# A selective scan in pairs of tiles: where a Mamba layer keeps its states, and in how many instructions it makes them

## The chip, the cores and the metric

The kernel runs on one core of a Trainium2 chip. The core has five engines that work side by side, each from its own queue in order: TensorE (PE, matrix products into PSUM), VectorE (DVE), ScalarE (ACT, functions such as Exp), GpSimd (POOL) and SyncE (SP, which here issues DMAs). PSUM has eight banks; one bank holds 512 f32 numbers for each of 128 partitions. The metric is the device time of one execution in microseconds (us). Times below are the median of several executions; a profile is of one execution.

## What is computed

The program is a stack of eight residual blocks over 32 sequences of 256 tokens with 128 features. The change touches the first block alone, a Mamba layer that runs in two directions (forward f, backward b). Cut to what matters here:

```python
xc = silu(causal_conv(in_proj(layernorm(x))));  z = ...
dt, Bm, Cm = split(xc @ xp_w.T)              # 16 states
delta = softplus(dt @ dtp_w.T + dtp_b);  A = -exp(A_log)
def step(h, inp):                            # h: 256 channels x 16 states
    dA = exp(d_t[..., None] * A)
    h = dA * h + (d_t * u_t)[..., None] * B_t[:, None, :]
    y = sum(h * C_t[:, None, :], axis=-1)
    return h, y
y = (y + xc * Dskip) * silu(z);  return y @ out_w.T
```

The backward direction does the same over the reversed sequence. All arithmetic is f32. The seven blocks behind it (two feed-forward blocks with experts, attention, and so on) are the same in both kernels.

## The kernel before

Tokens lie along the free axis, features along partitions. A chunk is 512 tokens (two sequences of 256), there are 16 chunks, and a chunk in one direction is a unit, so there are 32 units. The generator `unit` holds the whole work of one unit and gives up control at each `yield`; `pipeline` starts a new unit every 16 steps and moves all active units on by one step in turn, oldest first. A unit spends its first 24 steps on preparation (normalisation, convolution on PE, Silu, the projections, softplus by way of Abs, Exp and Ln, the gate) and then 16 steps on the recurrence, with three more to finish. So in any stretch of 16 steps one unit is in its recurrence while the next is being prepared.

256 channels times 16 states are 4096 rows, that is, 32 tiles of 128 partitions by 512 tokens. Two loops run over them: `h` (2 halves of the channels) and `g` (4 groups), and in a group `k` counts 4 tiles. For one tile:

- ACT makes the exponentials `dA` (L608), 510 of 512 elements. The first element of each of the two sequences stays zero, which resets the running state there. `dA` is one of three PSUM banks in turn (`dAs`, zeroed once at those places).
- POOL makes `dBu`, the product of delta times u (`widedu`) and B (L612), into one of four SBUF buffers.
- DVE runs the recurrence as one scan instruction (L621): state = dA * state + dBu along the 512 tokens.
- The states are multiplied by C. The states of tiles 0 and 1 lie side by side in a two-bank PSUM tile `h2`, and one DVE instruction multiplies both (L623, 1024 elements). Tile 2 uses `h2` again and is multiplied by DVE alone (L631). Tile 3 has its states in SBUF (`hs`), and POOL multiplies it (L569); all of the operands of POOL in this kernel lie in SBUF.
- PE sums four states to a channel with a 128x32 matrix (L574), one quarter of the output partitions for each `k`, into the one bank `yps`, after a first product with `skip` (L572). When a half is complete, `gated` multiplies `yps` by the gate on DVE (L590).

The PSUM banks of this stage are: 3 for `dAs`, 2 for `h2`, 2 for the preparation (`m`), 1 for `yps`.

What sets the order: the program is written as a sequence, and a planner (the tile framework) turns it into one queue for each engine. It keeps the data dependences and the reuse of buffers, sets the semaphores, and where an instruction is not ready by its own estimate it issues a later one of the same engine that is. `behind_scans` (through `issue_after`) keeps a few DVE instructions of the preparation and `gated` behind the last scan written. `summed` for group g is written after the second tile of group g+1, so the product of POOL stands in the text behind two further `dBu`. In step terms, one step holds two tiles.

SP issues the loads of the recurrence: `bc` (B and C, spread over partitions), and `wide` (delta and delta times u) in two halves, the first six steps ahead and the second at the second group of the first half.

## Time and profile before

| | us |
|---|---|
| median of 3 executions | 6238.78 (6236.38 to 6243.42) |
| the profiled execution | 6234.39 |
| its span, first to last instruction | 6232.7 |
| first scan starts / last scan starts (from the span's start) | 77.7 / 2052.8 |
| scans in that stretch | 1024, in 32 units |
| from one unit's first scan to the next one's, mean of units 2 to 31 | 62.06 |

How to read the profile's lines: a page has the busy time of each engine, then the span in 40 equal slices with the busy share in tenths. In a table of groups a row has the source line, the engine, the operation, what it writes and reads with shapes, the count, the total busy time and the mean duration in ns of one instruction, and then the idle time of its engine just ahead of it with what ended that idle time. A row of waits says which engine and tile waited for which, the total in us, how many times, and the longest. A row of the timeline has a start in us, a duration in us, and "x2" where two alike are merged. Durations on DVE and ACT overlap by a little where an instruction starts before the one ahead of it has quite ended.

### The profile page before, as it was taken

How to read it: one execution, taken by the hardware profiler on the slowest of the kernel's cores; microseconds unless marked ns; L12 is line 12 of the kernel's file. 1: busy time of each engine (PE TensorE's matmuls, PEld its weight loads, DVE VectorE, ACT ScalarE, POOL GpSimd, SP SyncE). 2: the span in 40 equal slices, each digit the busy share in tenths (PEclk: the TensorE clock that was granted, in tenths of full speed). 3: DMA queues.
4: the chain of work that ended last, by engine and by line, in shares of the span. 5: the costliest groups of instructions: out<-in, count | busy, mean ns of one | idle time of the engine just before them, and what ended most of it. 6: DMA issues, size and time to landing. Idle time of an engine off the chain costs nothing. (4 is left out here: it accounts for less than half of the span.)

```text
span 6232.7 us, 73938 instructions
## 1 busy us (share of the span) xinstructions
PE 5356.8 (86%) x25850; PEld 2792.6 (45%) x25922; DVE 4117.2 (66%) x7006; ACT 2710.2 (43%) x4424; POOL 3289.4 (53%) x3074
## 2 busy tenths in 40 slices
PE   6777777777777799999998888897998999997997
PEld 2222222222221466965544444445884444443886
DVE  5998999989989554044555555655665666665565
ACT  4665666666655354344434444342221333333221
POOL 5888888888888564044634444443332333333332
PEclk9888988888988899598989999998998999998998
DMA  3333333333332740000000000004550000000555
GB/s 148 123 123 116 123 116 123 116 123 116 126 112 109 304 185 1 1 1 1 1 1 10 9 8 8 11 8 129 186 172 19 20 16 18 18 11 12 188 188 189
DMA packets 190421, 512.13 MB, mean 82 GB/s; under 512 B 22177, under 2 KB 75169, under 8 KB 164961
## 3 DMA queue, kind: packets, MB, share of 16 engines
q1 hardware_dynamic: 172192, 468.00, 21.1%
q0 software_dynamic: 17280, 35.69, 1.7%
q8 instruction: 205, 3.36, 0.2%
q10 hardware_dynamic: 576, 3.71, 0.2%
q14 instruction: 168, 1.37, 0.1%
HBM read 359.93 MB, written 147.38 MB: 81 GB/s over the span
## 5 line engine op out<-in xcount | busy, mean ns | idle before, releaser
L612 POOL TENSOR_TENSOR dBu<-widedu,bcB 128x512 f32<-128x512 f32 x1024 | 1294.8, 1284 | 249.9 <-DVE h L621 162.0
L621 DVE TENSOR_TENSOR_SCAN h<-dA,dBu 128x512 f32<-128x512 f32 x768 | 942.5, 1227 | 119.8 <-ACT dA L608 30.4
L574 PE MATMUL yps<-pr,cst_t 128*32 128x512 f32 x2048 | 579.9, 645 | 244.8 <-POOL pr L569 102.7
L936 POOL TENSOR_SCALAR_AFFINE_SELECT e<-e 128x2048 f32<-128x2048 f32 (+1 forms) x256 | 343.3, 1353 | 597.2 <-ACT e L1047 386.1
L1412 POOL DMA_INDIRECT rows_out<-y,goes x284 | 271.8, 957 | 559.9 <-DVE y L1410 464.2
L1000 DVE TENSOR_REDUCE nm<-st 128x2 f32<-128x512 f32 x512 | 324.3, 684 | 268.5 <-PE st L996 267.4
L608 ACT ACTIVATE dA<-widedelta,Af 128x510 f32<-128x510 f32 x512 | 348.5, 688 | 300.9 <-DVE h L621 222.0
L608 ACT ACTIVATE dA<-widedelta,Ab 128x510 f32<-128x510 f32 x512 | 345.0, 686 | 272.7 <-DVE h L621 209.5
L1187 ACT ACTIVATE s<-s 128x512 f32<-128x512 f32 x284 | 179.0, 630 | 578.3 <-DVE s L1186 309.2
L574 PEld LDWEIGHTS yps<-pr,cst_t 128*32 128x32 f32 x2048 | 86.8, 112 | 704.8 <-POOL pr L569 228.0
L315 POOL TENSOR_TENSOR rstd<-var,cst_t 128x4 f32<-128x4 f32 x128 | 130.0, 1016 | 516.2 <-DVE var L313 514.4
L781 POOL TENSOR_TENSOR comb<-comb,ye 128x512 f32<-128x512 f32 x224 | 284.8, 1275 | 182.0 <-DVE ye L780 75.2
L1060 ACT ACTIVATE e<-st 128x512 f32<-128x512 f32 x512 | 272.0, 598 | 184.5 <-PE st L1056 154.8
L569 POOL TENSOR_TENSOR pr<-hs,bcC 128x512 f32<-128x512 f32 x256 | 334.4, 1306 | 13.7 <-DVE hs L621 13.7
L621 DVE TENSOR_TENSOR_SCAN hs<-dA,dBu 128x512 f32<-128x512 f32 x256 | 308.3, 1204 | 48.8 <-ACT dA L608 47.3
L1301 POOL DMA_INDIRECT rows_in<-xt,slot x256 | 253.6, 991 | 119.0 <-issue 98.7
L623 DVE TENSOR_TENSOR pr<-h,bcC 128x1024 f32<-128x1024 f32 x256 | 309.8, 1210 | 8.5 <-PE yps L574 0.5
L1188 DVE TENSOR_TENSOR hh<-s,u_ps 128x512 f32<-128x512 f32 x284 | 195.4, 688 | 172.0 <-ACT s L1187 168.0
L1393 PE MATMUL g_ps<-xb,gu 128*128 128x256 f32 x1136 | 302.6, 389 | 3.6 <-ACT xb L1376 2.3
L1402 PE MATMUL yps<-dn,hh 128*128 128x128 f32 x2272 | 291.5, 276 | 5.9 <-DVE hh L1188 5.8
L1393 PE MATMUL u_ps<-xb,gu 128*128 128x256 f32 x1136 | 293.3, 381 | 0.0
L1402 PEld LDWEIGHTS yps<-dn,hh 128*128 128x128 f32 x2272 | 282.8, 192 | 15.3 <-DVE hh L1188 7.8
(353 smaller groups left out, 11248.5 us busy)
## 6 DMA issues: line engine op xcount, KB each, us to landing
gu<-in_gu SPq DMA_DIRECT2D x142, 512.0 KB, 3.7
rows_in<-zero SPq DMA_DIRECT2D x60, 1170.0 KB, 18.7
widedelta<-delta_d SPq DMA_DIRECT2D x64, 1024.0 KB, 5.5
widedu<-du_d SPq DMA_DIRECT2D x64, 1024.0 KB, 5.1
dn<-in_dn SPq DMA_DIRECT2D x142, 256.0 KB, 3.9
bcB<-xdbl_d SPq DMA_DIRECT2D x32, 1024.0 KB, 5.0
bcC<-xdbl_d SPq DMA_DIRECT2D x32, 1024.0 KB, 6.9
xr<-rows_in SPq DMA_DIRECT2D x142, 130.0 KB, 3.8
```

Source lines behind the costliest of these rows:

```text
L569: nc.gpsimd.tensor_mul(pr, hs, bc["C"][:, g, :])
L574: nc.tensor.matmul(yps[32 * k : 32 * k + 32, :], K("states"), pr, start=False, stop=(g == 3), skip_group_check=True, tile_position=(0, 32 ...
L608: nc.scalar.activation(two(dA)[:, :, 1:L], two(steps)[:, :, 1:L], AF.Exp, scale=A[s][:, at : at + 1])
L612: nc.gpsimd.tensor_mul(dBu, duw[:, k, :], bc["B"][:, g, :])
L621: scan[0] = nc.vector.tensor_tensor_scan(*views, 0.0, ALU.mult, ALU.add)
L623: nc.vector.tensor_mul(pr2, h2, bc["C"][:, g, :].unsqueeze(1).to_broadcast([P, 2, CH]))
L781: nc.gpsimd.tensor_add(comb, comb, ye)
L936: nc.gpsimd.affine_select(e, e, [[0, n], [sign, P]], ALU.is_gt, 0.0, base=base, channel_multiplier=-sign)
L1000: nc.vector.tensor_reduce(n1[:, x, 2 * r : 2 * r + 2], o.rearrange("p (j k) -> p j k", j=2), AX.X, ALU.max, negate=True,)
L1060: nc.scalar.activation(e0[:, r], o.rearrange("p (j k) -> p j k", j=2), AF.Exp)
L1393: nc.tensor.matmul(o[:, j, :], gu[:, at : at + P], xb, start=True, stop=True)
L1402: nc.tensor.matmul(yps[:, t, :], hh[:, k, t * P : (t + 1) * P], dn[:, k, :], start=(k == 0), stop=(k == FF // P - 1),)
```

## The change

The recurrence goes over 16 pairs of tiles in a unit, one pair a step, instead of 32 tiles, two a step.

- `dAs` is two tiles of two banks each (4 banks), where it was three of one bank. ACT still makes the exponentials of each tile with an instruction of its own.
- One scan runs over both tiles of a pair, 1024 elements. For three pairs of four it writes the states over the exponentials in PSUM. The zeros at the four sequence starts are overwritten by that, so ACT writes them anew with a small copy (`firsts(dA)`, 128x4) ahead of the exponentials of each pair whose buffer was overwritten: 12 times in a unit.
- For the fourth pair (`i % 4 == 3`) the scan writes the states over `dBu` in SBUF, and POOL multiplies them by C in place, one instruction of 1024 elements, written one step later, behind the next pair's `dBu`.
- DVE multiplies the other three pairs of four, 1024 elements each, out of PSUM into one of three `prod` buffers. `h2`, `hs` and the single products are gone. So of a unit's tiles, DVE multiplies 24 and POOL 8, as before.
- `dBu` is made by one POOL instruction for a pair, into one of four buffers of 1024 elements.
- PE's sums of a pair are written two steps after it; `gated` three steps after the last pair of a half. `yps` has two banks, one for each half.
- In the backward direction the pair lies in reverse order in `dA`, the scan reads `dBu` backward, and the multiplication reads the states backward.
- The second half of `wide` is loaded at pair 2, the same step as before. The banks are now 4, 2 and 2.

```diff
--- before.py
+++ after.py
@@ -403,9 +403,14 @@
 
 
 
-        dAs = [ps.tile([P, CH], F32, name=f"dA{k}", bufs=1) for k in range(3)]
-        for t in dAs:
-            nc.vector.memset(two(t)[:, :, 0:1], 0.0)
+        dAs = [ps.tile([P, 2, CH], F32, name=f"dA{k}", bufs=1) for k in range(2)]
+        nought = wp.tile([P, 4, 1], F32, name="nought")
+        nc.gpsimd.memset(nought, 0.0)
+
+        def firsts(dA):
+            return dA.rearrange("p k (b t) -> p (k b) t", b=2)[:, :, 0:1]
+
+        nc.vector.memset(firsts(dAs[1]), 0.0)
 
         def rows_of(ap, at, dims, n_rows):
 
@@ -559,84 +564,81 @@
                 yield
 
 
-
-            sums, ended = None, None
-            yps = None
-
-            def summed(h, g, prods, hs):
-                nonlocal yps, ended
-                pr = p2.tile([P, CH], F32, tag="prod", name="pr", bufs=4)
-                nc.gpsimd.tensor_mul(pr, hs, bc["C"][:, g, :])
-                if g == 0:
-                    yps = ps.tile([P, CH], F32, tag="y", name="yps", bufs=1)
-                    nc.tensor.matmul(yps, skip[s][:, h, :], act[:, h, :], start=True, stop=False, skip_group_check=True)
-                for k, pr in enumerate([*prods, pr]):
+            due, yps = [], {}
+
+            def sum_up(i, prods):
+                h, first = i // 8, i % 8 == 0
+                if first:
+                    yps[h] = ps.tile([P, CH], F32, tag="y", name="yps")
                     nc.tensor.matmul(
-                        yps[32 * k : 32 * k + 32, :],
+                        yps[h], skip[s][:, h, :], act[:, h, :], start=True, stop=False, skip_group_check=True
+                    )
+                for k in range(2):
+                    at = 64 * (i % 2) + 32 * k
+                    nc.tensor.matmul(
+                        yps[h][at : at + 32, :],
                         K("states"),
-                        pr,
+                        prods[:, k, :],
                         start=False,
-                        stop=(g == 3),
+                        stop=(i % 8 > 5),
                         skip_group_check=True,
-                        tile_position=(0, 32 * k),
+                        tile_position=(0, at),
                     )
-                if g == 3:
-                    ended = h
-
-            def gated():
-                nonlocal ended
-                yg = p2.tile([P, CH], F32, tag=f"yg{s}{ended}", name="yg", bufs=1)
+
+            def gated(h):
+                yg = p2.tile([P, CH], F32, tag=f"yg{s}{h}", name="yg", bufs=1)
                 with behind_scans():
-                    nc.vector.tensor_mul(yg, yps, gate[:, ended, :])
-                outs[s, ended] = yg
-                ended = None
-
-            for h in range(2):
-                dw, duw = wide[h]
-                for g in range(4):
-                    if (h, g) == (0, 1):
+                    nc.vector.tensor_mul(yg, yps[h], gate[:, h, :])
+                outs[s, h] = yg
+
+            for i in range(19):
+                if i < 16:
+                    h, g, half = i // 8, i // 2 % 4, i % 2
+                    if i == 2:
                         wide.append(load(1))
-
-                    h2 = ps.tile([P, 2, CH], F32, tag="hs", name="h2", bufs=1)
-                    pr2 = p2.tile([P, 2, CH], F32, tag="prod2", name="pr2", bufs=2)
-                    prods = [pr2[:, 0, :], pr2[:, 1, :]]
-                    for k in range(4):
-                        dA = dAs[turn[0] % 3]
-                        turn[0] += 1
-                        at = 16 * h + 4 * g + k
-                        steps = dw[:, k, :] if s == "f" else dw[:, k, ::-1]
+                    dw, duw = wide[h]
+                    dA = dAs[i % 2]
+                    if i % 4 != 1:
+
+                        nc.scalar.copy(firsts(dA), nought)
+                    for k in range(2):
+                        at = 2 * i + k
+                        steps = dw[:, 2 * half + k, :]
+
+                        a = dA[:, k, :] if s == "f" else dA[:, 1 - k, :]
+                        steps = steps if s == "f" else steps[:, ::-1]
                         nc.scalar.activation(
-                            two(dA)[:, :, 1:L], two(steps)[:, :, 1:L], AF.Exp, scale=A[s][:, at : at + 1]
+                            two(a)[:, :, 1:L], two(steps)[:, :, 1:L], AF.Exp, scale=A[s][:, at : at + 1]
                         )
-                        dBu = p2.tile([P, CH], F32, tag="dBu", name="dBu", bufs=4)
-                        nc.gpsimd.tensor_mul(dBu, duw[:, k, :], bc["B"][:, g, :])
-                        if k == 3:
-                            hs = p2.tile([P, CH], F32, tag="hs", name="hs")
-                        elif k == 2:
-                            h2 = ps.tile([P, 2, CH], F32, tag="hs", name="h2", bufs=1)
-                            hs = h2[:, 0, :]
-                        else:
-                            hs = h2[:, k, :]
-                        views = (hs, dA, dBu) if s == "f" else (hs[:, ::-1], dA, dBu[:, ::-1])
-                        scan[0] = nc.vector.tensor_tensor_scan(*views, 0.0, ALU.mult, ALU.add)
-                        if k == 1:
-                            nc.vector.tensor_mul(pr2, h2, bc["C"][:, g, :].unsqueeze(1).to_broadcast([P, 2, CH]))
-                            yield
-                            if ended is not None:
-                                gated()
-                            if sums:
-                                summed(*sums)
-                        elif k == 2:
-                            pr = p2.tile([P, CH], F32, tag="prod", name="pr", bufs=4)
-                            nc.vector.tensor_mul(pr, hs, bc["C"][:, g, :])
-                            prods.append(pr)
-                    sums = (h, g, prods, hs)
-                    yield
-            yield
-            summed(*sums)
-            yield
-            gated()
-            yield
+                    dBu = p2.tile([P, 2, CH], F32, tag="dBu", name="dBu", bufs=4)
+                    nc.gpsimd.tensor_mul(
+                        dBu, duw[:, 2 * half : 2 * half + 2, :], bc["B"][:, g, :].unsqueeze(1).to_broadcast([P, 2, CH])
+                    )
+                    weights = bc["C"][:, g, :].unsqueeze(1).to_broadcast([P, 2, CH])
+
+                    hs = dBu if i % 4 == 3 else dA
+
+                    def flat(t, back=s == "b"):
+                        t = t.rearrange("p k t -> p (k t)")
+                        return t[:, ::-1] if back else t
+
+                    out = flat(hs) if i % 4 == 3 else flat(hs, False)
+                    scan[0] = nc.vector.tensor_tensor_scan(out, flat(dA, False), flat(dBu), 0.0, ALU.mult, ALU.add)
+                    if i % 4 == 3:
+                        prods = dBu
+                        due.append((i + 1, lambda t=dBu, w=weights: nc.gpsimd.tensor_mul(t, t, w)))
+                    else:
+
+                        states = dA if s == "f" else dA[:, ::-1, ::-1]
+                        prods = p2.tile([P, 2, CH], F32, tag="prod", name="pr", bufs=3)
+                        nc.vector.tensor_mul(prods, states, weights)
+                    due.append((i + 2, lambda i=i, t=prods: sum_up(i, t)))
+                    if i % 8 == 7:
+                        due.append((i + 3, lambda h=h: gated(h)))
+                for n, f in due:
+                    if n == i:
+                        f()
+                yield
             if s == "b":
                 m = pair()
                 for n, (q, h) in enumerate((q, h) for q in "fb" for h in range(2)):
```

## The prediction

> **What bounds the kernel now.** I read the page first, for the stage that the change touches.
>
> ```profile
> DVE  5998999989989554044555555655665666665565
> ACT  4665666666655354344434444342221333333221
> POOL 5888888888888564044634444443332333333332
> ```
>
> The recurrence fills the first 13 of the 40 slices. There DVE is at nine tenths, POOL at eight, ACT at six. Everything behind it is untouched, so what the stage gains or loses moves the end by the same amount. Next, the busy time of each engine in an even stretch of the stage (columns: PE, PEld, DVE, ACT, POOL), and the DVE groups in it:
>
> ```profile
> 300.00:2000.00 1700.00, 1284.11 (x3401) 371.82 (x3400) 1543.82 (x1464) 1046.98 (x1322) 1477.64 (x1151) 0.88 0.32 121
> ```
>
> ```profile
> L621 DVE TENSOR_TENSOR_SCAN h<-dA,dBu 128x512 f32<-128x512 f32 x659 | 808.7, 1227 | 87.7 <-ACT dA L608 29.1 <-POOL dBu L612 5.4 <-POOL pr L569 0.5
> L623 DVE TENSOR_TENSOR pr<-h,bcC 128x1024 f32<-128x1024 f32 x219 | 265.1, 1211 | 7.6 <-PE yps L574 0.5
> L621 DVE TENSOR_TENSOR_SCAN hs<-dA,dBu 128x512 f32<-128x512 f32 x219 | 263.8, 1204 | 44.7 <-ACT dA L608 44.7
> L631 DVE TENSOR_TENSOR pr<-h,bcC 128x512 f32<-128x512 f32 x219 | 150.7, 688 | 13.4 <-DVE h L621 0.5
> ```
>
> The stretch holds 1700 / 62.06 = 27.4 units. DVE is 91% busy, so it is the bound. What it waits for, and what ACT waits for, in the same stretch:
>
> ```profile
> ACT dA L608 <- DVE h L621: 359.8, 371, 3.2
> ...
> DVE hs L621 <- ACT dA L608: 44.7, 13, 4.5
> DVE h L621 <- ACT dA L608: 29.1, 33, 2.2
> DVE h L621 <- POOL dBu L612: 5.4, 9, 0.6
> ```
>
> ACT mostly waits for a free `dA` bank. DVE waits 83.7 us in all (these rows and four of 3.0 or less), 3.06 us a unit, and nine tenths of it is for exponentials. Last, the timeline, for how DVE passes from one instruction to the next:
>
> ```profile
> 1006.54 2.60 DVE L621 TENSOR_TENSOR_SCAN h<-dA,dBu 128x512 f32<-128x512 f32 x2
> 1009.05 1.20 DVE L621 TENSOR_TENSOR_SCAN hs<-dA,dBu 128x512 f32<-128x512 f32 x1
> 1010.16 1.20 DVE L623 TENSOR_TENSOR pr<-h,bcC 128x1024 f32<-128x1024 f32 x1
> ...
> 1036.39 1.23 DVE L621 TENSOR_TENSOR_SCAN h<-dA,dBu 128x512 f32<-128x512 f32 x1
> 1037.73 0.69 DVE L631 TENSOR_TENSOR pr<-h,bcC 128x512 f32<-128x512 f32 x1
> ```
>
> Two things are to be seen. The product at 1037.73 needs the scan ahead of it and starts 0.11 us after its end; the scan at 1009.05 and the product at 1010.16 need nothing of the instruction ahead and start 0.09 us before its end. And the planner uses that: it put the scan of tile 3 between the second scan and the product that waits for it. So it stands in 110 of 239 groups that I counted. ACT beside it:
>
> ```profile
> 1010.99 1.28 ACT L483 ACT_TABLE_LOAD   x1
> 1012.28 1.02 ACT L483 ACTIVATE act<-m 128x1024 f32<-128x1024 f32 x1
> 1013.32 1.28 ACT L608 ACT_TABLE_LOAD   x1
> 1014.62 1.30 ACT L608 ACTIVATE dA<-widedelta,Ab 128x510 f32<-128x510 f32 x2
> ```
>
> A Silu takes ACT away from the exponentials for 3.63 us, as it loads two function tables. A unit has three such blocks (Silu, Ln, gate), one of 1.9 us (Relu and Abs) and some four of 1.05.
>
> **The change, part by part, for one unit.**
>
> Scans. 32 of 1227 or 1204 ns (39.1 us) become 16 of 1024 elements, which no row shows. Upper bound: twice 1227, 2.454 us. Lower: one fixed part less. The two products (1211 at 1024, 688 at 512) give 1.02 ns an element and 166 ns fixed, so 2 x 1227 - 166 = 2.288 us. I take that, since the product is the nearest row on the same engine out of PSUM; 16 are 36.6 us. Writing into the bank that is read is in no row. A scan uses (1227 - 166) / 512 = 2.07 ns an element, the product 1.02, so there is time for a read and a write; I cost it at nothing, and keep one more access (1.02 ns an element, 1.05 us a scan) as the bad end.
>
> Products. Eight of 1211 and eight of 688 (15.2 us) become twelve of 1211 (14.5). Reading PSUM backward I cost at nothing: scans that write it backward take 1.228, forward ones 1.227.
>
> The rest of DVE is the same, 115 us of the stretch or 4.2 a unit. So DVE's work falls from 58.5 us to 55.3.
>
> The Trainium skill (VectorE: DVE Perf Modes, Rules for kernel authors, with the 150 cycles of setup in its side-by-side table) says to cut the count of instructions, since each pays that setup, some 0.156 us: for 20 fewer a unit an estimate of 3.1 us, or 99 over the stage. The rows here hide 0.09 of it wherever the next instruction is independent, which leaves 0.07, 1.4 us a unit or 45 in all.
>
> Handovers. As written, each product follows its own scan (+0.11) and each scan a product (-0.09): net nothing, 55.3. Where the planner issues scan, scan, product, product, nearly all 28 are independent: 55.3 - 28 x 0.08 = 53.0.
>
> Refill of `dA`, the wait that is added. Before, a bank was free when its scan ended, and there were three. Now a buffer is held through the product, and there are two. ACT then needs 0.04 us to start, the copy, two exponentials (1.31) and 0.09 until DVE starts. The copy, 128x4, is nearest to ACT's `rt_th` rows (0.20 us); behind another instruction less, at least 0.1 by my estimate: I take 0.15, so 1.59 us. Queued behind it on ACT are the second tile's exponentials, and the next unit's Silu, Ln and gate. As written, DVE covers that with the next scan (2.29) and its product, and only 0.6 to 1.9 us are spare. With scan, scan, product, product it is covered by one product alone (1.13): DVE stands 0.4 us, some eight times in a unit, 3.3.
>
> ACT's blocks. With the paired order ACT is idle some 4.3 us in a cycle of 7.2. A block of 3.63 that starts anywhere in it delays the refill by 3.63 x 3.63 / (2 x 4.3) = 1.5 us on average; three make 4.6, the smaller ones 0.9: 5.5. As written the same blocks cost about 1 us each beyond the spare time, 3.3 in all. The 3.06 of today goes away in either case, since it is the same wait.
>
> Sums: paired order 53.0 + 3.3 + 5.5 = 61.8; as written 55.3 + 3.3 = 58.6. The trace shows the planner passing the waiting product in about half of its chances, so I take the middle, 60.2 against 62.06: 1.86 us less. The stage is (2052.8 - 77.7) / 62.06 = 31.8 units: -59 us.
>
> POOL. 32 `dBu` every 1.23 us back to back and 8 products of 1.30 (49.8 us) become 20 instructions of 1024 elements; `du` of the same shape takes 2.36: 47.2. Cost nothing, as DVE hides it: POOL was waiting for DVE (207 us before `dBu`). If cover fails: written order puts the product of the fourth pair (2.36) and then a `dBu` (2.36) between the end of that scan and the scan after next, 4.7 us where DVE has 3.5 of work, 1.2 late four times a unit. Against it: now the planner runs `dBu` ahead of the product, behind the fourth `dBu` of the next group where the text has the second.
>
> PE's sums, 32 a unit, and `gated` are the same; two `yps` banks take away PE's wait for the gate, which DVE felt for 0.5 us in the stretch. SP issues the same loads in the same steps; `prod` is as many tiles deep as before. All cost nothing; PE is at 76%.
>
> The sum: 6234.4 (profiled) - 59 = 6175; the median stands 4 above the profiled execution: 6180.
>
> **The rivals.**
> 1. *As written throughout, the blocks hidden as now*: 55.3 + 3.06 = 58.4, -117 us, 6122. For it: the refill then has spare time. Against: the passed products.
> 2. *ACT's refill sets the pace; slower.* In the paired order nothing covers a block, so the three large ones count in full: 53.0 + 3.3 + 10.9 = 67.2, +163 us, 6402. It decides from the point where blocks cost more than 62.06 - 56.3 = 5.8 us a unit; my 5.5 is just below. For it: ACT is behind 88% of DVE's present wait. Against: three tiles of cover have kept that to 3.06.
> 3. *POOL's product of 1024 keeps its written place*: four pairs take 14.05 (4.7 + scans and products of the other three, 9.3) where DVE has 12.8: 56.2 + 4 + 3 = 63.2, +36 us, 6275.
> 4. *The longer scan saves nothing*: 16 x 0.166 = 2.7 on my 60.2, 62.9, +27, 6266. With the access on top, +17 a unit, +560.
>
> **How the numbers follow.** Main case 0.45, rival 1 0.13, rival 2 0.24, rival 3 0.10, rival 4 0.08 (0.02 for its bad end). Of the main case, whose own range of blocks and orders is 6130 to 6230, 0.36 is faster by over 0.2%, 0.05 within, 0.04 slower. 0.2% (12 us) is about what a measurement of this kernel can tell from no change. Faster 0.36 + 0.13 = 0.49; same 0.05 and 0.02 from rivals 3 and 4; slower the rest, 0.44. For 8 in 10 the range reaches from 6095, below rival 1, to 6370, short of rival 2's full price.
>
> **What would show it.** Scans of 2.29 us and DVE at 55 us busy a unit; DVE's groups of scans waiting on `dA` for 5 to 9 us a unit, ahead of the first scan behind two products; next to none on `dBu`. A scan well above 2.3, or waits on `dBu` of over 1 us four times a unit, would make the forecast wrong, and a wait on `dA` above 9 us would turn its sign.

## The result, and the profile after

The kernel after takes 6326.61 us (median of four executions, 6313.69 to 6330.52) against 6241.10 for the kernel before beside it: a ratio of 1.0127, with an interval of 1.0111 to 1.0144. The forecast was 6180 and faster; the sign is wrong, the time lies inside the range (6095 to 6370).

The page of the kernel after, busy tenths in 40 slices, and the even stretch of the stage (columns: PE, PEld, DVE, ACT, POOL, then the granted clock, the DMA share and GB/s):

```profile
DVE  4888888888888665134555555564665666664565
ACT  4666666656666355334433444442221333333221
POOL 4777777778787565124634444443332333333332
```

```profile
300.00:2000.00 1700.00, 1299.18 (x3282) 367.07 (x3282) 1413.75 (x880) 1052.47 (x1586) 1344.44 (x577) 0.83 0.30 114
```

DVE's digit went from nine to eight over the whole stage, POOL's from eight to seven, and ACT's stayed at six; behind the stage the digits are nearly the same but for the shift. The stretch of 1700 us now has 130 us less of busy DVE, and holds fewer units, 26.3 in place of 27.4. The groups of DVE, and what DVE and ACT wait for in that stretch:

```profile
L626 DVE TENSOR_TENSOR_SCAN dA<-dA,dBu 128x1024 f32<-128x1024 f32 x315 | 716.9, 2287 | 245.5 <-ACT dA L603 136.3 <-ACT dA L610 80.7 <-issue 18.4
L634 DVE TENSOR_TENSOR pr<-dA,bcC 128x1024 f32<-128x1024 f32 x316 | 381.5, 1218 | 17.0 <-DVE dA L626 0.9 <-PE yps L578 0.5
L626 DVE TENSOR_TENSOR_SCAN dBu<-dA,dBu 128x1024 f32<-128x1024 f32 x105 | 239.6, 2282 | 23.7 <-ACT dA L603 21.0 <-ACT dA L610 2.6
```

```profile
ACT dA L603 <- DVE pr L634: 441.6, 186, 5.2
...
DVE dA L626 <- ACT dA L603: 136.3, 52, 5.6
...
DVE dA L626 <- ACT dA L610: 80.7, 37, 2.5
...
ACT xdbl L496 <- PE m L494: 63.1, 26, 3.2
ACT delta L521 <- PE m L520: 50.4, 13, 4.1
```

The scan of 1024 takes 2.287 and 2.282 us, the product 1.218. DVE's waits for ACT are 136.3 + 80.7 + 21.0 + 2.6 = 240.6 us, 9.16 a unit, where they were 2.69. (The small copy L603 is named where it happens to end last; it stands ahead of the *next* pair's exponentials, and what DVE waited for are the exponentials in front of it.) Before `dBu` DVE hardly waits.

Laid out by unit, from DVE's own instruction records between the first scan of the third unit and that of the last (a *handover* is a step from one instruction to the next of under 0.2 us, below nothing where they overlap; a *long wait* is a gap above that):

| us in a unit | before | after | change |
|---|---|---|---|
| busy | 58.50 | 55.67 | -2.83 |
| handovers, net | 0.52 | -1.15 | -1.67 |
| long waits (how many) | 3.04 (2.4) | 10.19 (5.1) | +7.15 |
| from one unit to the next | 62.06 | 64.70 | +2.64 |

2.64 x 31.8 units are 84 us, and the medians differ by 85.5. So the change did to DVE's own work what it should, 4.50 us less in a unit, and then lost 7.15 to waits. Two of these, in the timeline (start, duration, and in brackets how long the engine stood idle before it):

```profile
1139.69 1.21 DVE L634 TENSOR_TENSOR pr<-dA,bcC 128x1024 f32<-128x1024 f32 x1
1140.00 0.69 ACT L610 ACTIVATE dA<-widedelta,Af 128x510 f32<-128x510 f32 x1
1140.24 1.80 PE L520 MATMUL m<-du,cst_t 128*128 128x512 f32 x2
...
1144.66 1.01 ACT L521 COPY delta<-m 128x1024 f32<-128x1024 f32 x1 [3.96 <-PE m L520]
1145.57 0.69 ACT L610 ACTIVATE dA<-widedelta,Af 128x510 f32<-128x510 f32 x1
1146.19 0.15 ACT L603 COPY dA<-nought 128x4 f32<-128x4 f32 x1
1146.35 2.30 DVE L626 TENSOR_TENSOR_SCAN dA<-dA,dBu 128x1024 f32<-128x1024 f32 x1 [5.45 <-ACT dA L603]
```

```profile
1104.64 0.69 ACT L610 ACTIVATE dA<-widedelta,Ab 128x510 f32<-128x510 f32 x1
1105.35 1.28 ACT L488 ACT_TABLE_LOAD   x1
1106.71 1.02 ACT L488 ACTIVATE act<-m 128x1024 f32<-128x1024 f32 x1
...
1107.75 1.28 ACT L610 ACT_TABLE_LOAD   x1
1109.04 0.69 ACT L610 ACTIVATE dA<-widedelta,Ab 128x510 f32<-128x510 f32 x1
...
1109.84 2.30 DVE L626 TENSOR_TENSOR_SCAN dA<-dA,dBu 128x1024 f32<-128x1024 f32 x1 [1.89 <-ACT dA L603]
```

In the first, ACT has made one exponential of a pair; its queue then holds the copy of `delta` for the next unit, which waits 3.96 us for PE, and only then the pair's other exponential. DVE stands for 5.45 us. In the second a Silu with its two table loads lies between the two exponentials. The scan needs both tiles, so whatever ACT does between them delays it in full, and the other pair buffer can't help: it is held until its product is done.

### The profile page after: what moved, and what is told of

Same layout as the page of the kernel before. It is cut to its first block, busy times and chain, and to the rows that moved or that the text cites. A ratio compares the mean times of both kernels' runs of the same rounds, so it can differ in the third digit from the quotient of the medians.

```text
span 6311.8 us, 72841 instructions
## 1 busy us (share of the span) xinstructions
PE 5422.4 (86%) x25922; PEld 2793.4 (44%) x25922; DVE 4035.8 (64%) x6364; ACT 2766.1 (44%) x4808; POOL 3205.6 (51%) x2435
## 5 line engine op out<-in xcount | busy, mean ns | idle before, releaser
L614 POOL TENSOR_TENSOR dBu<-widedu,bcB 128x1024 f32<-128x1024 f32 x512 | 1211.6, 2388 | 286.4 <-PE yps L578 181.1
L626 DVE TENSOR_TENSOR_SCAN dA<-dA,dBu 128x1024 f32<-128x1024 f32 x384 | 874.2, 2287 | 314.2 <-ACT dA L603 164.9
L578 PE MATMUL yps<-pr,cst_t 128*32 128x512 f32 x1536 | 432.7, 705 | 189.3 <-DVE pr L634 188.3
L634 DVE TENSOR_TENSOR pr<-dA,bcC 128x1024 f32<-128x1024 f32 x384 | 463.8, 1218 | 21.1 <-DVE dA L626 1.4
L629 POOL TENSOR_TENSOR dBu<-dBu,bcC 128x1024 f32<-128x1024 f32 x128 | 314.5, 2457 | 151.3 <-DVE dBu L626 151.3
L578 PE MATMUL yps<-dBu,cst_t 128*32 128x512 f32 x512 | 179.1, 786 | 221.8 <-POOL dBu L629 221.8
L626 DVE TENSOR_TENSOR_SCAN dBu<-dA,dBu 128x1024 f32<-128x1024 f32 x128 | 292.1, 2282 | 26.3 <-ACT dA L603 23.3
L603 ACT COPY dA<-nought 128x4 f32<-128x4 f32 x384 | 61.4, 160 | 548.2 <-DVE pr L634 547.3
```

The source lines that it names most:

```text
L578: nc.tensor.matmul(yps[h][at : at + 32, :], K("states"), prods[:, k, :], start=False, stop=(i % 8 > 5), skip_group_check=True, tile_positi ...
L614: nc.gpsimd.tensor_mul(dBu, duw[:, 2 * half : 2 * half + 2, :], bc["B"][:, g, :].unsqueeze(1).to_broadcast([P, 2, CH]))
L626: scan[0] = nc.vector.tensor_tensor_scan(out, flat(dA, False), flat(dBu), 0.0, ALU.mult, ALU.add)
L629: due.append((i + 1, lambda t=dBu, w=weights: nc.gpsimd.tensor_mul(t, t, w)))
L634: nc.vector.tensor_mul(prods, states, weights)
```

## The experiments

Three theories stand at the start. **A**: ACT's other work in its one queue meets too little cover, two pair buffers of which one is in the hands of DVE. **B**: the copy and the longer refill after each product set the pace. **C**: the paired order "scan, scan, product, product" leaves the refill bare. Later A was split: by its *sharpened* form what costs is that work comes between a pair's exponentials, by **A2** the small cover costs however ACT's queue is ordered. **P** says that ACT is late because PE is. Ratios are to the kernel before on the same chip; the kernel after stands at 1.0127. Expectations given in us were made for the chip of the result, where the kernel before takes 6241 us; on the chips of the other runs it takes 6243 to 6284, so compare ratios, or times of a unit: the chips differ mainly behind this stage, where the profiles show 4173 to 4243 us for the same program. All but four are made from the kernel after; those four say so.

**No copies.** The first tokens of a sequence get a large `delta` once `du` is made, so that the whole exponential is computed and is zero there by itself.

```diff
-                    if i % 4 != 1:
-                        nc.scalar.copy(firsts(dA), nought)
...
-                            two(a)[:, :, 1:L], two(steps)[:, :, 1:L], AF.Exp, scale=A[s][:, at : at + 1]
+                        nc.scalar.activation(a, steps, AF.Exp, scale=A[s][:, at : at + 1])
...
+            for h in range(2):
+                nc.gpsimd.memset(two(delta[:, h, :])[:, :, start : start + 1], 30000.0)
```

> The 12 small copies of zeros a unit are gone from ScalarE: GpSimd sets delta at the first token of each sequence to 30000 ahead of the store to DRAM, so that the exponential itself is 0 there, and ScalarE makes all 512 elements. The output is the same. Theory A (ScalarE's other blocks of work stand between the exponentials of a pair, and two buffers of a pair give too little cover): only the copies' own 12 x 0.16 us goes, partly out of idle time: 0.5 to 1.5 us a unit, 6280 to 6310. Theory B (the copy and the refill behind each product are themselves what VectorE waits for): its waits fall from 10.3 us a unit to about the 3 of before, 6100 to 6170.

Measured: 1.0087 [1.0059, 1.0115], a unit of 64.16, long waits 9.60. The twelve copies of 0.160 us are worth about half a us a unit, as A had it. So the copies are not the cause; the refill behind a product stays in this run, and what it is worth alone is in the table below.

**No table loads**, in the kernel after and in the kernel before: Exp in the place of Silu and Ln within `unit`, so the function values differ and the instructions are otherwise the same.

```diff
-            nc.scalar.activation(act, m, AF.Silu)
+            nc.scalar.activation(act, m, AF.Exp)
...
-            nc.scalar.activation(lg, one, AF.Ln, scale=-1.0)
+            nc.scalar.activation(lg, one, AF.Exp, scale=-1.0)
...
-            nc.scalar.activation(gate, m, AF.Silu)
+            nc.scalar.activation(gate, m, AF.Exp)
```

> Silu (twice) and Ln in the recurrence's unit are replaced by Exp, so ScalarE loads no function table there; this leaves out two Silus and the Ln of softplus, and the instructions stay. A block of 3.63 us becomes one of 1.05. Theory A: VectorE's waits fall by 5 to 7 us a unit, 6100 to 6170. Theory B: they stay, as the refill is the same; at most 1 us a unit, 6290 to 6325.

> The same replacement of Silu and Ln by Exp in the kernel before (it leaves out the same functions). Theory A: three buffers already hide most of the blocks, so at most 1 to 2 us a unit, 6175 to 6210. If the kernel before gains as much as the one after, the blocks are not what sets the two apart.

Measured: 0.9857 [0.9828, 0.9886] and 0.9867 [0.9836, 0.9897]. Without loads the two kernels are equal, 59.72 and 59.70 us a unit. The kernel after gains twice what the kernel before does (4.98 us a unit against 2.36, which is a little more than the 1 to 2 expected). Its waits of DVE, and those of the kernel before, both without loads (first fence the kernel after):

```profile
DVE dA L626 <- ACT dA L603: 106.2, 41, 5.7
DVE dA L626 <- ACT dA L610: 48.9, 35, 3.6
```

```profile
DVE hs L621 <- ACT dA L608: 8.4, 10, 2.0
```

With no load anywhere, three single buffers hide nearly everything (long waits 0.68 us a unit), and two pair buffers still leave 5.79. So of the 7.15 us, 5.79 - 0.68 = 5.11 are there without any load; the loads make the other 2.0. What they are made of can be read wait by wait in the traces, from what ACT did between the moment when the scan's buffer came free and the pair's last exponential:

| long waits, us in a unit | before | after | after, no loads |
|---|---|---|---|
| ACT stood for PE (0.2 us or more) | 0.47 | 5.60 | 4.17 |
| ACT loaded a table and did not stand for PE | 1.63 | 3.74 | 0 |
| other instructions of the preparation alone | 0.33 | 0 | 1.05 |
| nothing but exponentials and copy | 0.24 | 0.28 | 0.46 |
| not for exponentials | 0.37 | 0.57 | 0.11 |

Waits with loads grew by 2.1 us, waits with ACT standing for PE by 5.1, and the refill alone is nearly nothing, so B falls in its second half too. But ACT itself waits for PE no longer than it did. These are its waits for PE in the kernel before:

```profile
ACT sq L428 <- PE m L426: 56.1, 13, 5.3
ACT xdbl L491 <- PE m L489: 30.8, 13, 2.9
ACT delta L516 <- PE m L515: 22.4, 13, 2.0
...
ACT du L500 <- PE m L499: 20.6, 14, 3.5
```

With 5.9 us more before `act` they make 135.8 us, 4.96 a unit. In the kernel after the two rows shown above, 20.3 before `du` and 2.4 before `gate` make 136.2, 5.19 a unit. The standing was there before, though partly at other instructions; three single buffers hid it, two pair buffers don't.

**As written.** Each scan is issued behind the product before it, so that the paired order can't occur.

```diff
-                    scan[0] = nc.vector.tensor_tensor_scan(out, flat(dA, False), flat(dBu), 0.0, ALU.mult, ALU.add)
+                    with tc.issue_after(mul[0].ins) if mul[0] else nullcontext():
+                        scan[0] = nc.vector.tensor_tensor_scan(out, flat(dA, False), flat(dBu), 0.0, ALU.mult, ALU.add)
...
-                        nc.vector.tensor_mul(prods, states, weights)
+                        mul[0] = nc.vector.tensor_mul(prods, states, weights)
```

> The kernel after with every scan queued on VectorE behind the product of the pair ahead of it, so that scan, scan, product, product (45 of 359 scans) does not occur. Theory C (that paired order is what costs): 6230 to 6280. Theory A: within 15 us of the kernel after, 6310 to 6340, since the waits come from ScalarE's queue.

Measured: 1.0214 [1.0178, 1.025], long waits 11.50 (10.19). In the kernel after, "scan, scan, product, product" stands behind only 46 of the 384 scans into PSUM; here behind none, and it is worse. C falls. Theory A had expected no change (within 0.25%) and missed too: without the freedom to pass a waiting instruction DVE waits longer.

**ACT in the written order.** Each ACT instruction of preparation and recurrence is issued behind the one written before it, so nothing stands between a pair's exponentials; alone, and together with the zeros by `delta` and one step more for PE ahead of two of ACT's reads.

```diff
+        def on_act(f, *a, **k):
+            with tc.issue_after(acts[0].ins) if acts[0] else nullcontext():
+                acts[0] = f(*a, **k)
...
-            nc.scalar.activation(act, m, AF.Silu)
+            on_act(nc.scalar.activation, act, m, AF.Silu)
```

> The kernel after, with every ScalarE instruction of the recurrence's units queued in the order in which it is written, so that no Silu, Ln or gate block can stand between the two exponentials of a pair. Nothing else is changed. Theory A, sharpened (the planner's order puts blocks, and copies that wait for TensorE, between a pair's exponentials): VectorE's long waits fall from 10.2 us a unit to about 5, time 0.985 to 0.995 of before. Theory A2 (the place doesn't matter, two buffers are too few for 16 us of other ScalarE work whatever the order): 1.005 to 1.02.

> As the run with ScalarE in written order, and besides without the copies of zeros (zeros by data), and with one step between TensorE's matmuls and the ScalarE instruction that reads them in two places of the preparation (xdbl and the copy of delta). Theory A, sharpened: waits fall to 2 to 4 us a unit, 0.965 to 0.985 of before. Theory A2: 1.0 to 1.015.

Measured: 1.0074 [1.0053, 1.0094] and 1.0098 [1.0076, 1.012]; long waits 8.74 and 8.49. What ACT waits for in the first of them (ACT's instructions all show the helper's line):

```profile
ACT delta L404 <- PE m L526: 95.4, 26, 5.4
ACT xdbl L404 <- PE m L500: 92.1, 26, 5.3
```

In the kernel after, something of the preparation lies between the exponentials of 141 of 465 pairs, here of none. Pairs kept whole win back a fifth of the lost waits. The rest comes back in another place: ACT, no longer allowed to pass an instruction that waits, stands for 95.4 us where it stood for 50.4 before `delta`, 92.1 for 63.1 before `xdbl`. In both runs the expectation of the sharpened A missed and that of A2 was met; the sharpened A is at most a part.

**Two buffers in the kernel before**, the test of cover from the other side; nothing else is changed there.

```diff
-        dAs = [ps.tile([P, CH], F32, name=f"dA{k}", bufs=1) for k in range(3)]
+        dAs = [ps.tile([P, CH], F32, name=f"dA{k}", bufs=1) for k in range(2)]
...
-                        dA = dAs[turn[0] % 3]
+                        dA = dAs[turn[0] % 2]
```

> The kernel before with two banks for the exponentials instead of three; nothing else. If the depth of cover sets the price of a block, VectorE's long waits rise from 3.0 us a unit to 6 to 9, 1.015 to 1.03 of before. If only the place of the blocks in the queue does, under 1.005.

```profile
DVE h L621 <- ACT dA L608: 125.4, 76, 3.7
DVE hs L621 <- ACT dA L608: 26.3, 27, 2.3
```

Measured: 1.0103 [1.008, 1.0126], 64.35 us a unit. The two rows were 29.1 and 44.7; long waits went from 3.04 to 5.78. One bank less costs 2.7 us of waits a unit with no scan or product changed. That is cover alone, a little below what was expected of it. The unit grew by 2.29 us only, since `sp` (a DVE instruction of the preparation, see the last section) came out 0.46 shorter.

**A third pair buffer in the kernel after**, in SBUF since PSUM is full: it takes the exponentials of every fourth pair, whose states go to SBUF anyway. To make room, two `prod` buffers in place of three.

```diff
+        dAs.append(wp.tile([P, 2, CH], F32, name="dAs"))
...
-                    dA = dAs[i % 2]
-                    if i % 4 != 1:
+                    dA = dAs[2 if i % 4 == 3 else (i - i // 4) % 2]
+                    if i % 4 != 3:
...
-                        prods = p2.tile([P, 2, CH], F32, tag="prod", name="pr", bufs=3)
+                        prods = p2.tile([P, 2, CH], F32, tag="prod", name="pr", bufs=2)
```

> The kernel after with a third buffer of a pair for the exponentials, in SBUF, for the pair whose states go to SBUF; for room the product buffers are two, not three. Cover (A2): long waits fall from 10.2 us a unit to 4 to 6, 0.98 to 1.0 of before; VectorE's scan of that pair then reads two SBUF operands, which may lengthen GpSimd's products (0 to 2 us a unit). Order alone (A, sharpened): 1.005 to 1.015, since blocks still split pairs.

```profile
L627 DVE TENSOR_TENSOR_SCAN dA<-dA,dBu 128x1024 f32<-128x1024 f32 x291 | 662.8, 2285 | 154.5 <-ACT dA L611 154.5
L627 DVE TENSOR_TENSOR_SCAN dBu<-dAs,dBu 128x1024 f32<-128x1024 f32 x97 | 384.1, 3960 | 77.8 <-POOL dBu L615 68.8 <-ACT dAs L611 8.6
```

Measured: 1.0364 [1.0343, 1.0384]. Waits for exponentials did fall, to (154.5 + 8.6) x 69.73 / 1700 = 6.7 us a unit from 9.16. But a scan whose two inputs both lie in SBUF takes 3.960 us where the others take 2.285, and DVE's busy time rises by 6.2 us a unit. Where the time goes is seen in one of them:

```profile
1010.67 4.66 POOL L615 TENSOR_TENSOR dBu<-widedu,bcB 128x1024 f32<-128x1024 f32 x2 [1.05 <-PE yps L579]
...
1013.06 4.42 DVE L627 TENSOR_TENSOR_SCAN dBu<-dAs,dBu 128x1024 f32<-128x1024 f32 x1 [0.54 <-POOL dBu L615]
```

POOL's instruction ends at 1015.33, and the scan ends 2.15 us after that, about one whole scan: it stood still while POOL ran. The only one of the 128 such scans beside which POOL did nothing took 2.266 us, so two inputs in SBUF cost nothing by themselves. The Trainium skill (SBUF — State Buffer, Who interferes with whom) says the same: a DVE instruction with two SBUF inputs contends with a GpSimd instruction that reads SBUF, and whoever comes second is blocked until the other has ended. So this run doesn't measure what a third buffer would be worth without that.

**PE's sums one step later.** In the kernel after PE stands before sums whose products are not made, those of DVE and those of the fourth pair, which POOL makes; behind them in its queue stand the matrix products that ACT waits for.

```profile
PEld yps L578 <- DVE pr L634: 288.9, 170, 3.5
PEld yps L578 <- POOL dBu L629: 274.2, 105, 5.4
```

```diff
-                    due.append((i + 2, lambda i=i, t=prods: sum_up(i, t)))
+                    due.append((i + 3, lambda i=i, t=prods: sum_up(i, t)))
...
-                        due.append((i + 3, lambda h=h: gated(h)))
+                        due.append((i + 4, lambda h=h: gated(h)))
```

> The kernel after, with PE's sums of a pair and the gate written one step later (three steps behind the pair, the gate four), nothing else. Theory A (two buffers are too little cover for ScalarE's blocks; why a block is long matters little): PE's queue no longer stands at sums whose products are not made, but DVE still waits some 9 to 10 us a unit for exponentials; 1.009 to 1.014 of the kernel before (the kernel after stood at 1.0127). Theory P (the blocks are long because ScalarE waits for PE, and PE stands at sums that wait for DVE's products): the gaps beside the exponent of softplus, 5.3 us in two units without table loads, go away; DVE's long waits fall by some 2.5 us a unit, 2.5 x 31.8 = 80 us, 0.997 to 1.003.

Measured: 1.0051 [1.0031, 1.0071], 62.98 us a unit, long waits 7.92. The waits of PE's weight loads, of ACT and of DVE in this kernel:

```profile
PEld yps L578 <- POOL dBu L629: 275.3, 80, 5.4
PEld yps L578 <- DVE pr L634: 160.5, 128, 3.4
```

```profile
ACT delta L521 <- PE m L520: 6.0, 5, 1.2
```

```profile
DVE dA L626 <- ACT dA L610: 140.7, 81, 3.6
DVE var L445 <- PE m L442: 40.1, 13, 3.4
```

DVE's long waits fell by 2.27 us, as P had it (2.5); ACT's wait before `delta` went from 50.4 to 6.0 us. The waits for exponentials alone fell further, from 9.16 to 6.05 us a unit, but more than half of that came back elsewhere: 1.5 us a unit before `var`, a small DVE instruction of the normalisation that now waits for PE, and 0.35 by which `sp` got longer. The ratio stopped between the two expectations. The three that follow ask what this is worth together with the rest.

> The kernel after with PE's sums one step later, and in the Mamba layer Exp in the place of Silu and Ln (these two functions are left out, so that no table is loaded there). Without table loads alone the kernel after was at 0.9857 of the kernel before, with the sums later alone at 1.0051 (the kernel after itself 1.0127). If PE's lateness and the table loads make different waits, the gains add: 0.9857 - 0.0076 = 0.978, and DVE's long waits fall from 5.8 to some 3.5 us a unit. If both are the same waits, it stays at 0.983 to 0.987.

> The kernel after with PE's sums one step later, the zeros by a large delta in place of the copies, and ScalarE's queue kept in the written order, so that nothing stands between the two exponentials of a pair. With the order alone it was 1.0074 and ScalarE then waited for PE. If it did so because PE stood at sums, the order is now worth what the split pairs cost: 1.0051 - 0.004 (copies) - 0.005 (order) = 0.996, or below. If ScalarE's waits for PE come from the written order itself (PE has only a step of 4 us for its part), 1.000 to 1.007.

> The kernel after with PE's sums one step later and the zeros by a large delta in place of the copies. If the two gains add: 1.0127 - 0.0076 - 0.0040 = 1.001 (0.998 to 1.004). If they are the same waits: 1.004 to 1.008.

Measured: with no table loads 0.9863 [0.9833, 0.9893], the same as without the later sums (0.9857); with ACT in order and without copies 1.0205 [1.0174, 1.0236], worse than any of the three alone; without copies 1.0057 [1.0044, 1.0071], the same as with them. The gains do not add. In the run with ACT in order, ACT stands 164.9 us before `delta` (95.4 with the order alone). Each remedy takes away the waits that it names, and others take most of their place; without copies the long waits are 7.90 us a unit, with the copies 7.92. Without loads the later sums did take waits away (5.79 to 4.68 us a unit), but DVE's busy time rose by 0.58, about what `sp` grew by (1.570 to 2.184 us).

**A ring of five banks**, with one sum bank; a pair takes two banks in turn, on top of the kernel without copies; then also with the later sums.

```diff
-        dAs = [ps.tile([P, 2, CH], F32, name=f"dA{k}", bufs=1) for k in range(2)]
+        dAs = ps.tile([P, 5, CH], F32, name="dA", bufs=1)
...
-                    dA = dAs[i % 2]
+                    at0 = 2 * turn[0] % 5
+                    turn[0] += 1
+                    dA = dAs[:, at0 : at0 + 2, :] if at0 < 4 else dAs[:, ::-4, :]
...
-                    yps[h] = ps.tile([P, CH], F32, tag="y", name="yps")
+                    yps[h] = ps.tile([P, CH], F32, tag="y", name="yps", bufs=1)
```

> The kernel after with five PSUM banks for the exponentials in place of four, used as a ring in which a pair takes two in turn (one sum bank in place of two, zeros made by a large delta at the first tokens in place of the copies; every fifth pair lies in banks 4 and 0 and is scanned by two instructions of 512). Against the kernel without copies, 1.0087 of the kernel before. Theory A (cover decides): the first exponential of a pair no longer has to wait for the product of the pair before last, ScalarE may be one tile of 0.65 us and half a DVE cycle of some 1.7 us further ahead; DVE's long waits fall by 2 to 4 us a unit from 9.6, less 0.5 for the split scans: 0.985 to 1.000. Theory P (ScalarE's waits for PE decide, not the depth): the long waits stay at 8.5 to 9.6 us a unit, 1.006 to 1.012.

> The ring of five banks and the sums one step later together. Theory A: as the ring alone, within 0.3% of it. Theory P: below the ring alone by 0.8% or more, about 0.995 to 1.002. If both hold, the two gains add: 0.975 to 0.990, and the kernel beats both versions.

Measured: 1.1302 [1.1279, 1.1325] and 1.1274 [1.1251, 1.1297]. Not what was meant:

```profile
1005.13 2.30 DVE L632 TENSOR_TENSOR_SCAN dA<-dA,dBu 128x1024 f32<-128x1024 f32 x1 [1.54 <-ACT dA L611]
1007.53 1.23 DVE L640 TENSOR_TENSOR pr<-dA,bcC 128x1024 f32<-128x1024 f32 x1
1008.85 1.42 ACT L611 ACTIVATE dA<-widedelta,Af 128x512 f32<-128x512 f32 x2 [3.81 <-DVE pr L640]
```

The exponentials of a pair wait for the product of the pair just ahead, though they go to other banks; so it is for all 511 pairs that have one ahead. It seems that the five banks, being one tile, were ordered as one buffer. So the runs say nothing of five banks, but they price no cover at all: ACT and DVE take turns, and a unit takes 87.40 us, 31.51 of them waits. Whether a fifth bank would pay stays open.

**Fewer loads with the functions kept.** The Trainium skill (ScalarE: Activation LUTs, Table sets: the hidden batching unit) says that Tanh lies in the table set of Exp, so the two need no load between them. Silu is (tanh(x/2) + 1) * x/2. For `act` the weights are halved beforehand, so `m` is x/2 there, and the preparation gets one step more. This is done in the kernel after (sums later, no copies) and in the kernel before; then for the gate alone in both.

```diff
-            nc.scalar.activation(act, m, AF.Silu)
+            nc.scalar.activation(act, m, AF.Tanh)
+            with behind_scans():
+                nc.vector.scalar_tensor_tensor(act, act, 1.0, m, ALU.add, ALU.mult)
+            yield
...
-            nc.scalar.activation(gate, m, AF.Silu)
+            nc.scalar.activation(gate, m, AF.Tanh, scale=0.5)
+            half_z = both("sp", 1)
+            nc.scalar.mul(half_z, m, 0.5)
+            nc.gpsimd.tensor_mul(gate, gate, half_z)
+            nc.gpsimd.tensor_add(gate, gate, half_z)
```

> The kernel after with PE's sums one step later, zeros by a large delta in place of the copies, and both Silu as (tanh(x/2) + 1) * x/2, Tanh being in the table of Exp: two of the three blocks of a unit load no table any more. The first is finished by one DVE instruction of 1024 (1.22 us), the gate by a copy on ScalarE and two GpSimd instructions. If table loads against too little cover are the cost: 1.001 for later and copies together, less two thirds of 4.4 us a unit (2.9), plus 1.22 on DVE, 1.7 x 31.8 = 54 us: 0.990 to 0.995, faster than both versions. If GpSimd's 4.8 us a unit or the longer chain take it back: 1.000 to 1.010.

> The kernel before with the same two Silu by Tanh. Its table loads cost 2.4 us a unit in all, so two thirds are 1.6; DVE has 1.22 more: 0.996 to 1.000. GpSimd is busy 87% of this stage and gets 4.8 us a unit more, 95%: if it becomes the bound, 1.005 to 1.02. In any case the gain is smaller than that of the same edit in the kernel after.

> As the run before, with the gate's Silu alone by Tanh (a copy on ScalarE, two GpSimd instructions; no instruction on DVE, and nothing of the preparation waits for the gate). One block of three loads no table any more. If a block costs a third of what all loads cost, 1.4 us a unit, 1.4 x 31.8 = 45 us: 0.7% below the run without it. If it was the loads' place in the chain of the preparation that cost, not their number, within 0.3% of the run without it; if GpSimd's 4.8 us more a unit become the bound, 0.5% or more above it.

> The kernel before with the gate's Silu alone by Tanh. A third of the loads' 2.4 us a unit, 0.8 x 31.8 = 25 us: 0.996. GpSimd goes from 87% to some 95% of the stage: if it then holds DVE up, 1.005 to 1.015.

The table rows of the kernel before, and of the kernel before with Tanh, in the stretch:

```profile
L608 ACT ACT_TABLE_LOAD x81 | 103.9, 1283 | 1.4
L483 ACT ACT_TABLE_LOAD x27 | 34.6, 1283 | 0.5
L507 ACT ACT_TABLE_LOAD x27 | 34.6, 1283 | 0.5
L536 ACT ACT_TABLE_LOAD x27 | 34.6, 1283 | 0.5
```

```profile
L617 ACT ACT_TABLE_LOAD x27 | 34.6, 1283 | 0.5
L512 ACT ACT_TABLE_LOAD x26 | 33.4, 1283 | 0.5
```

The rule holds: six loads a unit became two, 1.283 us each (the page's example gives some 2.7 for one). The time did not follow. With both Silu the kernel after is at 1.006 [1.0039, 1.0081], where it was at 1.0057 without Tanh, and the kernel before at 1.0162 [1.0126, 1.0197]; for the gate alone they are at 1.0141 [1.0125, 1.0156] and 1.0165 [1.0151, 1.0179], both slower than without. In the kernel before with the gate alone, DVE has no instruction more; its busy time is 58.47 us a unit, as before. Its waits:

```profile
DVE h L625 <- ACT dA L612: 68.6, 38, 4.7
DVE var L440 <- PE m L437: 54.5, 13, 4.4
DVE h L625 <- POOL dBu L616: 22.8, 15, 1.8
```

Some 39 us (with 16.3 of another row) are for POOL, as the rival said, but 54.5 are for PE, at `var`, which has no row among DVE's waits in either kernel. In this program's order it stands ahead of scans before its input is made; why the planner put it there is open. In the kernel after with the gate alone the long waits rose by 2.0 us a unit (7.90 to 9.90), and nearly all of it is of this kind: `var` waits 66.9 us in the stretch where it waited 36.9, and `xin`, its neighbour, 18.6, while the waits for POOL are below 1 us. There GpSimd's work is not what cost. No kernel here beats both versions with its functions kept.

## Why the prediction was wrong, step by step

- **Scans: right.** 2.288 us worked out from the slope of the products, 2.287 and 2.282 measured; a scan that writes where it reads costs nothing more. Rival 4 is refuted.
- **Products: right.** 1.211 taken, 1.218 measured, backward ones included. DVE's busy time was to fall from 58.5 to 55.3; it fell to 55.67, and `sp`, longer by 0.31, is most of the difference.
- **Handovers: order misjudged, size right by luck.** The paired order was put at half; it stands behind 46 of 384 scans. Net handovers came to -1.15 us a unit, the middle of the forecast's two cases (0 and -2.24), because the written order is cheaper than "net nothing": it has -0.80 where it is kept throughout. DVE without waits is 54.52, against the forecast's middle of 54.15.
- **Refill and copy: present, small.** 3.3 us a unit in the paired order, halved in the middle; waits with nothing but exponentials and copy measure 0.28, the copies are worth some 0.5, and the paired order is rare. As for its size on ACT, 0.15 was taken and 0.160 measured.
- **ACT's blocks: this is the step that failed.** "As written the same blocks cost about 1 us each beyond the spare time, 3.3 in all" and "5.5" in the paired order. Waits for exponentials measure 9.16 us a unit in an order that is mostly as written, and 11.50 in long waits where it is wholly so. In the middle, the forecast had 6.05 of waits in all against 10.19 of long waits: 4.14 of the 4.5 us by which the unit was missed; the rest is DVE's own 0.37.
- What the step left out: it counted three blocks with loads and small single instructions, each as if ACT then went on. For these its size was about right: waits with a load and no standing for PE are 3.74 us a unit, where its middle had 4.4 for all blocks. What it put at nothing, without a reason, is ACT standing in its own queue for PE (63.1 + 50.4 us before `xdbl` and `delta`, 4.3 us a unit), although the trace of before had as much of it: 5.60 us a unit of DVE's long waits contain such a standing, and 5.11 of the 7.15 us stay without loads. It also let a block fall ahead of or behind a pair's exponentials, never between them, and keeping pairs whole is worth 1.45 us of waits.
- "The 3.06 of today goes away in either case, since it is the same wait": true as bookkeeping, but the same wait had been kept at 3.06 by three buffers. One fewer in the kernel before costs 2.7.
- **Rival 2 is what happened**, by its consequence (ACT sets the pace, slower) and in size between the main case and its full price: 64.70 a unit, where it had 67.2. Its condition was wrong in one point: the paired order isn't needed, and without it things are worse. Its point of decision, blocks above 5.8 us a unit, was passed; so was the 9 us on `dA` that the prediction named as turning its sign.
- **POOL: right.** DVE waits for `dBu` in hardly any row, so rival 3 did not occur; POOL itself waits for PE (147.5 us before `dBu`), which the step didn't have.
- **PE's sums, "cost nothing": wrong.** Written two steps behind their pair, they stop PE's queue, and a step later gives back 0.76% of the time.

What is settled: the loss is wait for exponentials, and less cover alone, with no other change, makes such waits (2.7 us a unit in the kernel before). Of the 7.15 us, loads make 2.0 and the rest is there without them, most of it with ACT standing for PE as long as it always did. The reverse is not shown: no run gives the kernel after more cover without another change. Not settled is a sum of shares: lateness of PE (2.3 by the run with later sums), order within a pair (1.45), copies (0.6) and loads (4.4 as measured on the kernel after alone) overlap, as the combined runs show, and a small edit can also move the planner's order elsewhere by as much, as at `var`.

## What to carry to other kernels

Before joining two instructions of the bounding engine, count buffers in time, not in bytes: how long can the producer be away before the consumer stands, with the buffer held through its *last* reader. Then list everything in the producer's in-order queue that could make it late, its own waits for others included, since after the change those waits are the bound's. And price remedies in combination: here three that each took 0.4 to 0.8% off gave, two or three at a time, no more than the best of them, or a loss.

## What the hardware showed that was not expected

- A scan with both inputs in SBUF beside a busy GpSimd: 3.960 us against 2.285 with one input in PSUM. `sp`, the only large DVE instruction of the preparation with two SBUF inputs, varies with its place, perhaps for the same reason, which was not tested: 1.678 us on average in the kernel before, 1.984 in the kernel after, 2.333 with the later sums, whose DVE is busier by that (56.04 against 55.67 us a unit). In the run with a buffer in SBUF, keeping the exponentials in PSUM would have been worth more than the buffer.
- The granted clock of PE over the stretch was 0.88 in the kernel before and 0.83 in the kernel after, and without table loads 0.91 and 0.83, where both are equally fast and PE runs the same 3470 or so matrix products. So at the same rate of work the kernel after was granted less. The records hold 1.0 and 0.5 alone, and the mean is their mixture: a unit of the kernel after has 21.8 us at 0.5, one of the kernel before 15.3. In the wait of 5.45 us shown above PE had stood 4.46 us for POOL's product; the clock was 0.5 from 1134.98 to 1141.80, and PE's weight loads for `delta` followed each other at 0.86 us, and at 0.43 once it was 1.0. So a part of that wait is PE at half clock. Why the kernel after has more such stretches isn't known, and whether they have a share in the loss was not tested; that ACT's waits for PE are as long in total in both kernels speaks against a large one. In the ring, where PE runs 2428 products, the mean was 0.73.
